# A graph layer with 64 experts on one core: degree counting over 320 rows in place of 444, a first expert pass of 48 node tiles, expert sizes in steps of 16

## The chip, the cores and the metric

The kernel runs on one core of one Trainium2 chip. The metric is the device time of one execution in microseconds (us); less is better. Engines are named as in the profile: PE is TensorE's matrix unit (PEld its weight loads), DVE is VectorE, ACT is ScalarE, POOL is GpSimd, and SP is SyncE, which here only issues DMAs. An indirect DMA that POOL issues fetches or stores 128 rows of a tensor in HBM by a list of 128 indices.

## The reference

There are 12,500 nodes with 256 features, and 212,500 edges, sorted by their destination. The layer sums each node's neighbours (with weights from the degrees), passes the sum and the node through two matrices, sends each node to the two best of 64 experts, adds what these return, normalizes each column over all nodes, adds the input and normalizes each row.

```python
def _forward(feats, W_gc, b_gc, W_res, b_res, Wg, bg, w1, b1, w2, b2, gamma, beta, src, dst):
    deg_out = jnp.clip(segment_sum(ones, src), 1.0)
    deg_in = jnp.clip(segment_sum(ones, dst), 1.0)
    h = feats * rsqrt(deg_out)[:, None]
    m = segment_sum(h[src], dst) * rsqrt(deg_in)[:, None]
    x = m @ W_gc + b_gc + feats @ W_res + b_res            # 12500 x 256
    vals, idx = top_k(x @ Wg + bg, 2); gates = softmax(vals)
    # expert e on its nodes: gelu(x @ w1[e] + b1[e]) @ w2[e] + b2[e],  w1: 256x512, w2: 512x256
    y = x + sum of gate * expert(x) over the node's two experts
    return (y - mean(y, 0)) * rsqrt(var(y, 0) + eps) * gamma + beta
result = layernorm(x + _forward(x, ...))
...
```

All matrix products are in float32; only counts and comparisons are in bfloat16.

## The kernel before

**Start.** The degrees by destination are counted from the sorted list, the features are scaled by them and written to HBM as `h_d`. Before that, POOL makes constants: `lane_b`, `diff`, ..., then `from_a` by one iota for each distinct size in `TOKENS_A`, then `cen`, a block of zeros and `place`, from which DVE makes the first keys.

**Edges, in rows.** A row is 128 edges; there are `MC` = 1596. For each, POOL gathers 128 rows of `h_d` into one of 20 places of a ring (`row`, L763, the DMA on L767), DVE makes a 128x128 matrix of ones and zeros from the destinations (`one_hot`, L759, twelve rows ahead), and PE multiplies the two (L784). Twelve rows make a group, which is copied (L819), transposed (L834) and added to the sums `acc` (L857). All other work of this stage is put between the rows by hand: `at_row(c, f)` puts f behind row c, `later` puts it some rows on, `spread` distributes a list. So the order on every engine is fixed when the program is built, and each engine works through its own list in order. The stage is in two pieces: `go(0, CA)` with `CA` = `PA` x 12 = 528 rows, and, behind a branch that is not taken with these inputs, `go(CA, MC)`.

**Counting.** Within the first piece the out-degrees are counted, to see that they equal the in-degrees (the graph is symmetric). The 68 steps lie between row `COUNT_FROM` = 30 and `COUNT_TO` = `CA` - 54. Each step is two large comparisons on DVE (`compare` and `compare_b`, which call `hot`, L237), eight sign instructions on ACT (L1454) and 25 small matmuls on PE (L1459 and L1463, in lots of five rows). The comparisons write into two buffers in turn, so step k waits for the matmuls of step k-2. Between rows 62 and 281 DVE also packs lists of edges (`squeezing`).

**Node chains.** From row `CA` on, `begin_nodes` starts a chain for each two tiles of 128 nodes whose sums are complete, at least `BETWEEN` = 12 rows apart: dense product (L929, L934), best two experts, ranks among the nodes of an expert, and entries into the expert's list (L1062, into the PSUM tile `tab`). The expert outputs of the first `TA` = 44 tiles ("A nodes") come from pass A, those of the other 54 ("B nodes") from pass B. A nodes are written to `xa_d`, B nodes to `xb_d`.

**Pass A.** When the chains of the A nodes are through, `pass_a` sorts the experts by their number of nodes and spreads their work over the rest of the rows, up to `END_A` - 20 = row 1564. `TOKENS_A` has, for the 64 ranks, a size in units of `TU` = 32 nodes that the expert of that rank is taken to have; if an expert had more, a slow path would run. `parts_a` cuts sizes over `MOST_A` = 224 into parts. For each tile of 128: a gather on POOL (L1236), a transposition (L1249), the hidden layer (L1272, gelu L1283), the product (L1300), and a store to `oa_d`. Both passes use 128 columns of PE per tile however few nodes the last tile has.

**Pass B** comes after the last row, in an order that the framework's scheduler sets. `pieces_of(TOKENS_B, 4)` cuts each expert into parts of at most 4 tiles. For each part: POOL gathers the tiles (`gather`, L1696), PE transposes them (L1711), DVE copies that (L1715), PE makes the hidden layer (L1724, 16 records a part), ACT the gelu (L1728), PE the product (L1751, 8 records a tile), DVE adds the bias and scales (L1756, L1761), and POOL stores each tile to `z_d` (L1762). Gathers run three parts ahead (`AHEAD`). The weights of an expert are 1 MB, loaded into one of three buffers (L1686). Beside the first 44 parts stand the A nodes: for each tile, two gathers from `oa_d` (`added`, L1784) that DVE adds in (L1790), and every four tiles a transposition (L1800). `order_of` sorts the experts for either pass; among its small instructions are DVE memsets that lay out the sizes.

**End.** The B nodes' outputs are read back from `z_d` in units of four tiles (`NODES_B`, L1926) and added on PE (L1945, L1947) with the statistics on DVE (L1953). Then come the normalization and the stores.

Of the kernel before, what the change touches and what calls it, by code (L numbers as in the profile page):

```python
# [19 lines left out]
P = 128  # L20
# [34 lines left out]
LAST = M - HE - (NL - 1) * L  # L55
PA = 44
CA = PA * GR
# [24 lines left out]
def last_node(g):  # L82
    return min(center(g) + SL, N - W)


TU = 32

TA = 44
NA = TA * P
ZR = NP - NA  # L90
TOKENS_A = [
    13, 12, 11, 10, 10, 9, 9, 9, 9, 8, 8, 8, 8, 8, 8, 8, 8, 7, 7, 7, 7, 7, 7, 7, 7, 6, 6, 6, 6,
    6, 6, 6, 6, 5, 5, 5, 5, 5, 5, 5, 5, 5, 5, 5, 5, 5, 4, 4, 4, 4, 4, 4, 4, 4, 4, 4, 3, 3, 3, 3,
    3, 3, 3, 3,
]
TOKENS_B = [
    16, 15, 14, 13, 13, 12, 12, 11, 11, 10, 10, 10, 10, 10, 10, 9, 9, 9, 9, 9, 9, 8, 8, 8, 8, 8,
    7, 7, 7, 7, 7, 7, 7, 7, 7, 7, 6, 6, 6, 6, 6, 6, 6, 5, 5, 5, 5, 5, 5, 5, 5, 5, 4, 4, 4, 4, 4,
    4, 4, 4, 4, 4, 4, 4,
]  # L100
MOST_A = 7 * TU
RPE = CAP // P
# [38 lines left out]
def gnn_moe_kernel(  # L141
# [209 lines left out]
    for b in sorted(set(TOKENS_A), reverse=True):  # L351
        n = TOKENS_A.count(b)
        GP.iota(
            from_a[:, a : a + n], pattern=[[b * TU, n]], base=sum(TOKENS_A[:a]) * TU,
            channel_multiplier=0, allow_small_or_imprecise_dtypes=True,
        )
# [739 lines left out]
    parts_a = pairs_of(TOKENS_A, MOST_A)  # L1096
    END_A = MC - 12

    def order_of(one, total, sizes, ord_p, exp, over):
# [12 lines left out]
        V.tensor_add(pos[:, 0:1], pos[:, 0:1], pos[:, 1:2])  # L1112
        V.tensor_scalar(perm, lane[:E, :E], pos[:, 0:1], None, op0=ALU.is_equal)
        V.tensor_copy(pos[:, 0:1], part[:E])
        V.tensor_scalar_min(pos[:, 1:2], cnt, float(CAP))
        for k in range(2):
            T.matmul(ord_p[:, k], pos[:, k : k + 1], perm, start=True, stop=True)
        V.tensor_copy(exp[:, 0], ord_p[:, 0])
        V.tensor_scalar_mul(exp[:, 1], ord_p[:, 0], float(RPE))
        room, more = one([1, E]), one([1, E])  # L1120
        at = 0
        for b in sorted(set(sizes), reverse=True):
            V.memset(room[:, at : at + sizes.count(b)], float(b * TU))
            at += sizes.count(b)
        V.tensor_tensor(more, ord_p[:, 1], room, op=ALU.is_gt)
        V.tensor_reduce(over, more, axis=AX.X, op=ALU.add)
        return junk, cnt, perm
# [5 lines left out]
    def pass_a(t):  # L1133
# [7 lines left out]
        def one(shape):  # L1141
# [5 lines left out]
        junk, cnt, perm = order_of(  # L1147
            one, total_a, TOKENS_A, shut(t)[:1, : 2 * E].rearrange("p (k e) -> p k e", k=2),
            exp_a, over_a,
# [474 lines left out]
    with tc.manual_schedule(engines=EVERY):  # L1624
# [42 lines left out]
    order_of(  # L1667
        lambda shape: one.tile(shape, F32, name=f"ord{next(names)}"), total, TOKENS_B,
        banks[0][:1, : 2 * E].rearrange("p (k e) -> p k e", k=2), exp_b, over_b,
# [5 lines left out]
    with ExitStack() as stack:  # L1675
# [29 lines left out]
        def turn(xg):  # L1705
# [3 lines left out]
            for k in range(n):  # L1709
                for c in range(2):  # L1710
                    T.transpose(  # L1711
                        xtp[:, c, k * P : (k + 1) * P], xg[k][:, c * P : (c + 1) * P], ident
                    )
            xT = two.tile([P, 2, 4 * P], F32, name="xT")
            V.tensor_copy(xT[:, :, : n * P], xtp[:, :, : n * P])  # L1715
            return xT

        def hidden(w, xT, m):
            w1 = w[:, : 2 * H].rearrange("p (c h) -> p c h", h=H)
            h1 = two.tile([P, 4, 4 * P], F32, name="h1")  # L1720
            for j in range(4):
# [142 lines left out]
        with tc.If(nc.values_load(over_n[0:1, 0:1]) > 0):  # L1864
            with tc.For_i(0, E, 1) as e:
                w, bb = load(e)
                at = two.tile([P, RPE], I32, name="at")
                V.tensor_copy(at, slot_a[:, bass.ds(e * RPE, RPE)])
                for b in range(0, RPE, 4):
                    h1 = hidden(w, turn(gather(at[:, b : b + 4], 4, xa_d)), 4 * P)  # L1870
                    for k, r, yo in products(w, bb, h1, 4 * P):
                        nc.sync.dma_start(og_d[bass.ds(e * CAP + (b + k) * P, P)], yo)
# [19 lines left out]
            with tc.For_i(0, E, 1) as e:  # L1892
# [4 lines left out]
                V.tensor_copy(second, snd[:, bass.ds(e * RPE, RPE)])  # L1897
                for b in range(0, RPE, 4):
                    g = gather(at[:, 0, b : b + 4], 4)
                    gb = gates_of(g, second[:, b : b + 4])  # L1900
                    outputs(w, bb, at[:, 1, b : b + 4], gb, hidden(w, turn(g), 4 * P), 4 * P)

# [201 lines left out]
```

## Time and profile before

| | |
|---|---|
| median of 3 runs | 3065.71 us (3063.93 to 3073.05) |
| the profiled execution | 3071.5 us, of which the span from first to last instruction is 3069.7 us |
| granted TensorE clock over the span | 0.936 |
| busy | PE 2510.7 us (82%), PEld 1867.0 (61%), DVE 1644.5 (54%), ACT 729.5 (24%), POOL 2048.1 (67%) |
| first gather of a row, last gather of a row | 97.38 us, 2299.11 us |
| first matmul of the hidden layer in pass B | 2355.92 us |

So the span has four stretches: the start up to 97 us, the rows up to 2299 us, pass B up to 2901 us, and the end. A line of a group has the line of the program, engine, operation, what is written and read, and the count; then busy time and the mean duration in ns of one; then the idle time of the engine just before such instructions and what ended it. The matmuls' ends are modelled, so two neighbours may overlap in a timeline; from the start of one to the start of the next is the pace. Each matmul instruction in float32 shows as two records. A line of windows has the stretch, its length, the busy time and count of each engine, the granted clock, the share of the DMA engines and GB/s.

### The profile page before, as it was taken

The page shows a single profiled execution, that of the slowest core. Times are in us where ns is not written, and L with a number is a line of the kernel's source. Part 1 is how long each engine was busy: PE and PEld are TensorE (multiplying, and loading weights), DVE is VectorE, ACT ScalarE, POOL GpSimd, SP SyncE. Part 2 cuts the span into 40 slices and gives each one's busy share as a digit, 9 for nine tenths or more (in the row PEclk, how much of TensorE's full clock was granted, in tenths as well). Part 3 has the DMA queues.
Part 4 walks back from the last instruction along what each step waited for, and adds up shares of the span by engine and source line. Part 5 has one row for each costly group of instructions (what it writes and reads, how often), then busy time and mean ns, then how long its engine had stood idle before and what let it go on. Part 6 is the DMA issues. An engine that isn't in the chain of part 4 may idle for free. (4 is left out here: it accounts for less than half of the span.)

```text
span 3069.7 us, 42189 instructions
## 1 busy us (share of the span) xinstructions
PE 2510.7 (82%) x12984; PEld 1867.0 (61%) x13053; DVE 1644.5 (54%) x6062; ACT 729.5 (24%) x2126; POOL 2048.1 (67%) x2114
## 2 busy tenths in 40 slices
PE   2477777777688887899998988999895899989895
PEld 2254455454465554667777766677772577877795
DVE  8567775554378776454444343444455544444247
ACT  2023334331111111222222122122220121222246
POOL 0577777777777777777777777777774667765200
PEclk9979988997799998999999999999997999999998
DMA  8833333344565555556666777777864566787768
GB/s 282 253 95 102 103 101 107 109 114 116 183 189 150 146 141 156 153 178 184 193 193 201 203 211 196 209 229 239 252 204 129 166 209 206 252 258 230 259 208 277
DMA packets 288735, 566.53 MB, mean 185 GB/s; under 512 B 56759, under 2 KB 194967, under 8 KB 280307
## 3 DMA queue, kind: packets, MB, share of 16 engines
q0 software_dynamic: 99728, 271.07, 30.8%
q1 hardware_dynamic: 175063, 279.59, 28.8%
q10 hardware_dynamic: 13708, 13.06, 1.4%
q8 instruction: 107, 1.75, 0.2%
q14 instruction: 129, 1.06, 0.1%
HBM read 495.77 MB, written 67.76 MB: 184 GB/s over the span
## 5 line engine op out<-in xcount | busy, mean ns | idle before, releaser
L767 POOL DMA_INDIRECT ring<-h_d,src_col x1596 | 1565.0, 981 | 577.8 <-issue 428.2
L784 PE MATMUL p<-ring,o 128*128 128x257 f32 (+1 forms) x3192 | 1054.3, 432 | 311.2 <-DMA ring<-h_d,src_col 257.8
L784 PEld LDWEIGHTS p<-ring,o 128*128 128x128 f32 x3192 | 565.3, 205 | 544.3 <-DMA ring<-h_d,src_col 328.9
L759 DVE TENSOR_SCALAR o<-lane,rel 128x128 f32<-128x128 f32 x1596 | 399.5, 297 | 224.7 <-PE p L784 223.7
L1283 ACT ACTIVATE acc<-p,acc 128x128 f32<-128x128 f32 (+4 forms) x332 | 128.3, 387 | 734.2 <-PE p L1272 451.8
L237 DVE TENSOR_TENSOR acc<-bank,acc 125x2450 bf16<-125x2450 bf16 (+1 forms) x136 | 185.1, 1361 | 197.0 <-PE bank L1459 189.6
L1751 PE MATMUL yp<-w,h 128*128 128x256 f32 (+3 forms) x1136 | 263.9, 383 | 17.8 <-DVE yo L1756 17.8
L1307 DVE TENSOR_TENSOR acc<-yp_a,acc 128x256 f32<-128x256 f32 (+3 forms) x120 | 50.2, 418 | 426.2 <-PE yp_a L1300 422.8
L1272 PE MATMUL p<-acc 128*128 128x128 f32 (+4 forms) x1328 | 238.1, 302 | 4.6 <-ACT s L819 0.9
L1724 PE MATMUL hp<-xT,w 128*128 128x128 f32 (+12 forms) x1024 | 227.2, 374 | 15.2 <-DVE xT L1715 14.1
L1272 PEld LDWEIGHTS p<-acc 128*128 128x128 f32 x1328 | 209.4, 193 | 47.5 <-ACT acc L1283 25.5
L1300 PE MATMUL yp_a<-acc 128*128 128x256 f32 (+3 forms) x960 | 236.7, 391 | 0.0
L1751 PEld LDWEIGHTS yp<-w,h 128*128 128x128 f32 (+3 forms) x1136 | 189.7, 174 | 70.8 <-DVE yo L1756 21.9
L1454 ACT ACTIVATE acc<-lane_b,acc 125x128 bf16<-125x128 bf16 x544 | 168.3, 389 | 239.0 <-PE bank L1463 149.3
L1728 ACT ACTIVATE h<-hp,w 128x128 f32<-128x128 f32 (+12 forms) x256 | 117.2, 460 | 393.1 <-PE hp L1724 334.6
L1724 PEld LDWEIGHTS hp<-xT,w 128*128 128x128 f32 x1024 | 171.4, 194 | 63.0 <-issue 25.3
L1762 POOL DMA_INDIRECT z_d<-yo,tables x142 | 137.8, 971 | 94.0 <-DVE gate L1738 37.6
L1300 PEld LDWEIGHTS yp_a<-acc 128*128 128x128 f32 (+3 forms) x960 | 164.0, 175 | 47.0 <-issue 8.4
L1696 POOL DMA_INDIRECT xg<-xb_d,tables x142 | 137.2, 966 | 72.4 <-PE xtp L1711 33.9
L819 ACT COPY s<-p 128x257 f32<-128x257 f32 (+1 forms) x133 | 49.7, 374 | 491.6 <-PE p L784 401.0
L1459 PEld LDWEIGHTS <-acc 125*128 125x128 bf16 x1156 | 86.9, 105 | 102.2 <-issue 59.1
L1236 POOL DMA_INDIRECT acc<-xa_d,tables x120 | 114.9, 958 | 36.6 <-issue 30.2
(350 smaller groups left out, 3205.1 us busy)
## 6 DMA issues: line engine op xcount, KB each, us to landing
w<-in_wpack SPq DMA_DIRECT2D x64, 1026.0 KB
acc<-in_wpack SPq DMA_DIRECT2D x128, 512.0 KB
ring<-h_d,src_col POOLq DMA_INDIRECT x1596
tables<-h_d SPq DMA_DIRECT2D x105, 128.0 KB
zt<-z_d SPq DMA_DIRECT2D x26, 512.0 KB
acc<-acc_d SPq DMA_DIRECT2D x14, 896.0 KB
xt<-in_x ACTq DMA_DIRECT2D x48, 256.0 KB
z<-in_x SPq DMA_DIRECT2D x12, 1024.0 KB
```

What stands on the lines that cost most here:

```text
L237: V.tensor_tensor(o.rearrange("p k (a b) -> p k a b", b=2), lane_b[:p, None, :n] .rearrange("p k (a b) -> p k a b", b=2) .to_broadcast([p, ...
L759: o_last[u] = V.tensor_scalar(o_of[u][:, j], lane, rel[:, c : c + 1], None, op0=ALU.is_equal)
L767: i = GP.indirect_dma_start(out=r[:, k, :D], out_offset=None, in_=h_d, in_offset=bass.IndirectOffsetOnAxis(ap=src_col[:, c : c + 1], axis=0),)
L784: i = T.matmul(p_of[g][:, :n], o_of[v][:, m], r[:, k, :n], start=j == 0, stop=j == GR - 1)
L1272: T.matmul(hp, w1[:, c, j * P : (j + 1) * P], xT[:, c, :m], start=c == 0, stop=c == 1,)
L1283: S.activation(h1[:, j, :m], hp_of.pop((q, j)), AF.Gelu, bias=b1_a[i % 2][:, j : j + 1])
L1300: T.matmul(y, h1[:, j, k * P : k * P + n], w2[:, j], start=j == 0, stop=j == 3)
L1454: S.activation(s_los[k % 2][:, j], lane_b[:EP], AF.Sign, bias=nbs[u % 2][:, i, j : j + 1])
L1696: GP.indirect_dma_start(out=g, out_offset=None, in_=of, in_offset=bass.IndirectOffsetOnAxis(ap=at[:, k : k + 1], axis=0),)
L1724: T.matmul(hp[:, :m], w1[:, c, j * P : (j + 1) * P], xT[:, c, :m], start=c == 0, stop=c == 1,)
L1751: T.matmul(yp[:r], h1[:, j, k * P : k * P + r], w2[:, j], start=j == 0, stop=j == 3,)
L1762: st = GP.indirect_dma_start(out=z_d, out_offset=bass.IndirectOffsetOnAxis(ap=at[:r, k : k + 1], axis=0), in_=yo[:r], in_offset=None,)
```

## The change

- `PA` goes from 44 to 34, and so `CA` from 528 to 408. Counting lies between rows 30 and 354, and the branch and the first node chains come at row 408.
- `TA` goes from 44 to 48 tiles, so there are 6144 A nodes in place of 5632, and 50 B tiles in place of 54. `END_A` - 20 is row 1596, the end of the rows, in place of 1564.
- `TU` goes from 32 to 16, with new tables of sizes. `TOKENS_A` sums to 12,944 places (12,448 before) for 12,288 entries (11,264 before), in 90 parts and 127 tiles (83 and 120). `TOKENS_B` sums to 13,344 places (15,232) for 12,712 entries (13,736), in 66 parts and 129 tiles (64 and 142).
- Pass B's parts have at most 3 tiles (`WIDE`), not 4, and its tiles `xT` and `h1` shrink with that. An expert with four tiles is now cut into two and two.
- The sizes for the test on overflow are laid out by POOL at the start, into the new tile `room` (38 small memsets), in place of DVE memsets in `order_of`. POOL's `from_a` takes 18 iotas in place of 11.
- The slow path works in lots of 2 tiles in place of 4; it does not run with these inputs.

```diff
-PA = 44
+PA = 34
-TU = 32
-TA = 44
+TU = 16
+TA = 48
 TOKENS_A = [
-    13, 12, 11, 10, 10, 9, 9, 9, 9, 8, 8, 8, 8, 8, 8, 8, 8, 7, 7, 7, 7, 7, 7, 7, 7, 6, 6, 6, 6,
...
+    26, 24, 23, 22, 21, 19, 19, 18, 18, 17, 17, 17, 17, 17, 16, 16, 16, 16, 15, 15, 15, 15, 15,
...
 TOKENS_B = [
-    16, 15, 14, 13, 13, 12, 12, 11, 11, 10, 10, 10, 10, 10, 10, 9, 9, 9, 9, 9, 9, 8, 8, 8, 8, 8,
...
+    27, 25, 23, 23, 22, 21, 20, 19, 18, 18, 18, 18, 17, 17, 17, 16, 16, 16, 16, 15, 15, 15, 15,
...
-MOST_A = 7 * TU
+MOST_A = 14 * TU
+WIDE = 3
...
+    room = route.tile([1, 2, E], F32)
...
+    for k, sizes in enumerate((TOKENS_A, TOKENS_B)):
+        for b in set(sizes):
+            a, n = sizes.index(b), sizes.count(b)
+            GP.memset(room[:, k, a : a + n], float(b * TU))
...
-    END_A = MC - 12
+    END_A = MC + 20
...
-        room, more = one([1, E]), one([1, E])
-        at = 0
-        for b in sorted(set(sizes), reverse=True):
-            V.memset(room[:, at : at + sizes.count(b)], float(b * TU))
-            at += sizes.count(b)
+        more = one([1, E])
...
-            xT = two.tile([P, 2, 4 * P], F32, name="xT")
+            xT = two.tile([P, 2, WIDE * P], F32, name="xT")
-            h1 = two.tile([P, 4, 4 * P], F32, name="h1")
+            h1 = two.tile([P, 4, WIDE * P], F32, name="h1")
-        parts = pieces_of(TOKENS_B, 4)
+        parts = pieces_of(TOKENS_B, WIDE)
```

The lines of the changed program lie 2 to 6 further on: L767 is L773 there, L784 is L790, L1236 is L1238, L1272 is L1274, L1300 is L1302, L1696 is L1698.

Where the instructions stand, first on POOL from the last gather of pass A to the first store of pass B. Before (`ring` is a row, `acc<-xa_d` a tile of pass A, `xg` a tile of pass B, `co` a tile of A outputs, `z_d` a store):

```order
L1236 DMA acc<-xa_d,tables 128x258
L767 DMA ring<-h_d,src_col 128x256 x59
L1638 IOTA rank 128x512
L1643 IOTA to 128x512
L1784 DMA co<-oa_d,pos_a 128x256 x3
L1696 DMA xg<-xb_d,tables 128x258 x17
L1784 DMA co<-oa_d,pos_a 128x256 x3
L1696 DMA xg<-xb_d,tables 128x258 x4
L1784 DMA co<-oa_d,pos_a 128x256 x3
L1762 DMA z_d<-yo,tables 79360x256
```

And after the change:

```order
L1238 DMA acc<-xa_d,tables 128x258
L773 DMA ring<-h_d,src_col 128x256 x27
L1640 IOTA rank 128x512
L1645 IOTA to 128x512
L1786 DMA co<-oa_d,pos_a 128x256 x3
L1698 DMA xg<-xb_d,tables 128x258 x11
L1786 DMA co<-oa_d,pos_a 128x256
L1698 DMA xg<-xb_d,tables 128x258 x3
L1786 DMA co<-oa_d,pos_a 128x256 x2
L1698 DMA xg<-xb_d,tables 128x258 x3
L1786 DMA co<-oa_d,pos_a 128x256 x4
L1764 DMA z_d<-yo,tables 78336x256
```

The last gather of pass A has moved from row 1537 to row 1569 (its first from row 855 to row 903), and the first store of pass B stands behind 27 DMAs of that pass in place of 30, because its first part has two tiles in place of four.

Second, PE behind the last dense product of two tiles, where the last rows are multiplied. Before, nothing of pass A is left there (`p` written from `ring` comes from a row; `bank` belongs to the node chain):

```order
L934 MATMUL bank_122<-wcat,xT 128x320 x2
L784 MATMUL p_123<-ring,o 128x257 x2
L996 LDWEIGHTS before
L996 MATMUL bank_121<-both,before 128x64
L997 LDWEIGHTS ones_b
L997 MATMUL bank_121<-both,ones_b 128x64
L996 LDWEIGHTS before
L996 MATMUL bank_122<-both,before 128x64
L997 LDWEIGHTS ones_b
L997 MATMUL bank_122<-both,ones_b 128x64
L784 MATMUL p_123<-ring,o 128x257 x2
```

After the change the hidden layer (L1274) and the products (L1302) of pass A stand between these rows:

```order
L940 MATMUL bank_123<-wcat,xT 128x320 x2
L790 MATMUL p_124<-ring,o 128x257
L1302 MATMUL yp_a<-acc 96x256 x4
L1274 MATMUL p_125<-acc 128x96 x2
L790 MATMUL p_124<-ring,o 128x257
L1002 LDWEIGHTS before
L1002 MATMUL bank_122<-both,before 128x64
L1003 LDWEIGHTS ones_b
L1003 MATMUL bank_122<-both,ones_b 128x64
L1002 LDWEIGHTS before
L1002 MATMUL bank_123<-both,before 128x64
```

One product of pass A, four matmuls of 96 rows, now stands behind the very last row.

More of the change, by code (lines that the diff above doesn't have):

```diff
@@ L91 @@
 TOKENS_A = [
-    13, 12, 11, 10, 10, 9, 9, 9, 9, 8, 8, 8, 8, 8, 8, 8, 8, 7, 7, 7, 7, 7, 7, 7, 7, 6, 6, 6, 6,
-    6, 6, 6, 6, 5, 5, 5, 5, 5, 5, 5, 5, 5, 5, 5, 5, 5, 4, 4, 4, 4, 4, 4, 4, 4, 4, 4, 3, 3, 3, 3,
-    3, 3, 3, 3,
[3 rows of a table added]
 ]
 TOKENS_B = [
-    16, 15, 14, 13, 13, 12, 12, 11, 11, 10, 10, 10, 10, 10, 10, 9, 9, 9, 9, 9, 9, 8, 8, 8, 8, 8,
-    7, 7, 7, 7, 7, 7, 7, 7, 7, 7, 6, 6, 6, 6, 6, 6, 6, 5, 5, 5, 5, 5, 5, 5, 5, 5, 4, 4, 4, 4, 4,
-    4, 4, 4, 4, 4, 4, 4,
-]
-MOST_A = 7 * TU
[3 rows of a table added]
+]
+MOST_A = 14 * TU
+WIDE = 3
 RPE = CAP // P
@@ L1096, in gnn_moe_kernel, with order_of @@
     parts_a = pairs_of(TOKENS_A, MOST_A)
-    END_A = MC - 12
-    def order_of(one, total, sizes, ord_p, exp, over):
+    END_A = MC + 20
+    def order_of(one, total, room, ord_p, exp, over):
         junk, cnt, pos, perm = one([E, E]), one([E, 1]), one([E, 2]), one([E, E])
@@ L1147, in pass_a @@
         junk, cnt, perm = order_of(
-            one, total_a, TOKENS_A, shut(t)[:1, : 2 * E].rearrange("p (k e) -> p k e", k=2),
+            one, total_a, room[:, 0], shut(t)[:1, : 2 * E].rearrange("p (k e) -> p k e", k=2),
             exp_a, over_a,
@@ L1667, in gnn_moe_kernel @@
     order_of(
-        lambda shape: one.tile(shape, F32, name=f"ord{next(names)}"), total, TOKENS_B,
+        lambda shape: one.tile(shape, F32, name=f"ord{next(names)}"), total, room[:, 1],
         banks[0][:1, : 2 * E].rearrange("p (k e) -> p k e", k=2), exp_b, over_b,
@@ L1868, in gnn_moe_kernel @@
                 V.tensor_copy(at, slot_a[:, bass.ds(e * RPE, RPE)])
-                for b in range(0, RPE, 4):
-                    h1 = hidden(w, turn(gather(at[:, b : b + 4], 4, xa_d)), 4 * P)
-                    for k, r, yo in products(w, bb, h1, 4 * P):
+                for b in range(0, RPE, 2):
+                    h1 = hidden(w, turn(gather(at[:, b : b + 2], 2, xa_d)), 2 * P)
+                    for k, r, yo in products(w, bb, h1, 2 * P):
                         nc.sync.dma_start(og_d[bass.ds(e * CAP + (b + k) * P, P)], yo)
@@ L1897, in gnn_moe_kernel @@
                 V.tensor_copy(second, snd[:, bass.ds(e * RPE, RPE)])
[L1898 to L1901, printed above, removed]
+                for b in range(0, RPE, 2):
+                    g = gather(at[:, 0, b : b + 2], 2)
+                    gb = gates_of(g, second[:, b : b + 2])
+                    outputs(w, bb, at[:, 1, b : b + 2], gb, hidden(w, turn(g), 2 * P), 2 * P)
     with ExitStack() as stack:
```

4 rows, old and new, of tables (TOKENS_A, TOKENS_B) are left out of this document.

## The prediction

> **What bounds the kernel now.** I read the windows first, to see which engine has no time to spare in each stretch, then the timeline at the seams, then the groups by form for durations. Two windows of the rows and two of pass B:
>
> ```profile
> core 0: us, PE busy (x) PEld busy (x) DVE busy (x) ACT busy (x) POOL busy (x), PEclk, DMA share, GB/s
> ...
> 300.00:400.00 100.00, 73.37 (x467) 48.93 (x466) 72.83 (x166) 32.20 (x103) 76.22 (x79) 0.90 0.36 103
> ...
> 2000.00:2100.00 100.00, 93.39 (x463) 70.19 (x467) 41.11 (x195) 22.60 (x71) 76.10 (x79) 0.98 0.73 215
> ...
> 2500.00:2600.00 100.00, 97.17 (x443) 70.75 (x442) 43.60 (x114) 20.49 (x40) 70.98 (x74) 1.00 0.68 206
> ...
> 2700.00:2800.00 100.00, 93.54 (x493) 78.65 (x492) 43.61 (x113) 24.78 (x58) 63.69 (x66) 0.98 0.75 240
> ```
>
> POOL issues 79 gathers in each 100 us of the rows, early and late. Its 76 us "busy" looks like spare time, but is none: the group of the gathers and the timeline at the last of them say why.
>
> ```profile
> L767 POOL DMA_INDIRECT ring<-h_d,src_col x1596 | 1565.0, 981 | 577.8 <-issue 428.2 <-DVE o L759 91.7 <-PE p L784 14.9
> ```
>
> ```profile
> 2297.86 0.94 POOL L767 DMA_INDIRECT ring<-h_d,src_col  x1 [0.30 <-issue]
> ...
> 2299.11 0.95 POOL L767 DMA_INDIRECT ring<-h_d,src_col  x1 [0.30 <-issue]
> ...
> 2309.51 1.05 POOL L1638 IOTA rank<- 128x512 f32 x1 [9.46 <-PE p L784]
> ```
>
> One gather takes 0.95 us and 0.30 us of issue: 1.25 us from start to start. 1596 + 120 of them are 2145 us of the 2202 us from first to last (97.38 to 2299.11). Nothing but "issue" holds POOL up for long, so the rows are bound by the number of gathers. In pass B, PE is busy for 93 to 97 us in 100, but POOL with 74 DMAs is near its 80 too.
>
> **The change part by part.** The profiled execution took 3071.5 us, 5.8 above the median of 3065.7; I sum differences and set them off against the median.
>
> *The start.* POOL's seven more iotas and 38 memsets stand ahead of `place`, for which DVE's first key waits.
>
> ```profile
> 0.25 0.10 POOL L2091 MEMSET const-float32-0.0<- 128x1 f32 x1 [0.25 <-issue]
> 0.28 0.10 POOL L2091 MEMSET const-float32-1.0<- 128x1 f32 x1
> ...
> 2.01 1.08 POOL L353 IOTA from_a<- 64x1 f32 x11
> ...
> 3.76 1.95 POOL L388 IOTA rel<- 125x1716 bf16 x1
> ```
>
> ```profile
> 6.59 1.93 DVE L418 SCALAR_TENSOR_TENSOR lines<-lines,rel 125x1700 f32<-125x1700 int32 x1 [5.00 <-DMA lines<-in_dst]
> ```
>
> Iotas: 7 x 0.098 = 0.7 us. Memsets start 0.03 us apart and last 0.10, so 38 are 1.1 to 3.8 us. `place` is ready at 5.71 and the key starts at 6.59 on a DMA, so 0.9 us are covered: +0.9 to +3.6; I take +1, since successive memsets overlap in these rows. The DVE memsets that go from `order_of` were placed in a wait and give nothing.
>
> *Counting in 324 rows, not 444.* The same 68 steps. DVE's share is the question, because in rows 62 to 281 `squeezing` runs beside it.
>
> ```profile
> L237 DVE TENSOR_TENSOR acc<-bank,acc 125x2450 bf16<-125x2450 bf16 (+1 forms) x47 | 64.0, 1362 | 52.1 <-PE bank L1459 49.6 <-PE bank L1463 2.1
> ```
>
> That is 64.0 of DVE's 145 busy us in the 200 us from 200 to 400. The steps come 6.53 / 4.76 = 1.37 times as densely, which adds at most 0.37 x 64 / 2 = 12 us and about 1 us of digits per 100: DVE goes from 73 to 86, and PE likewise. Both stay below 100, and the ring's 20 rows (25 us) cover short delays. I take 0 for it; if DVE falls behind, the price is among the rivals. The early branch lets 15 chains start 120 rows sooner, and nobody waits for them: POOL's pace does not depend on it.
>
> A gather can be held up by DVE:
>
> ```profile
> 135.25 1.71 POOL L767 DMA_INDIRECT ring<-h_d,src_col  x1 [0.30 <-issue]
> 137.26 3.98 POOL L767 DMA_INDIRECT ring<-h_d,src_col  x1 [0.30 <-PE p L784]
> ```
>
> The second lasts 3.0 us longer than the normal 0.95. If such losses went by the row, 120 fewer rows of counting would give some back: counting shows about 79 gathers per 100 us where 80 would fit, so 1% of 150 us, -1.5 us. If they go by the DVE instruction, it is 0, since no comparison is removed. I take 0. The Trainium skill (SBUF — State Buffer, "Who interferes with whom") says that a DVE instruction in a two-port mode and GpSimd block each other for a whole instruction; by that rule the loss goes by the instruction, so the sum has 0 and not -1.5. The long gather above agrees with it in kind.
>
> *Pass A with 127 tiles.* Seven more gathers on POOL, where the rows are bound: 7 x 1.25 = +8.8 us. PE's part of pass A grows by 6% and is spread over 666 rows, not 682 (last and first gather), so its density per row grows by 8%. From 1300 to 2250:
>
> ```profile
> L784 PE MATMUL p<-ring,o 128*128 128x257 f32 x1260 | 378.2, 397 | 75.5 <-DMA ring<-h_d,src_col 54.7 <-ACT ring L779 16.1 <-ACT acc L1283 3.2
> L1300 PE MATMUL yp_a<-acc 128*128 128x256 f32 (+3 forms) x886 | 219.2, 392 | 0.0
> L1272 PE MATMUL p<-acc 128*128 128x128 f32 (+4 forms) x1196 | 217.4, 305 | 4.2 <-ACT s L819 0.9 <-ACT acc L1283 0.3
> ```
>
> 8% of 437 us is 35 us in these 950, and PE waits 75.5 us there for rows: it still has slack, and POOL stays the bound. 0 beyond the gathers.
>
> *The end of the rows.* Pass A now runs to the last row. Before, it was over at 2285, and PE then worked off rows that lay ready:
>
> ```profile
> 2286.43 2.33 PE L784 MATMUL p<-ring,o 128*128 128x257 f32 x10
> ...
> 2288.82 5.38 PE L784 MATMUL p<-ring,o 128*128 128x257 f32 x24
> ```
>
> 34 records are 17 rows, done in 7.7 us where POOL takes 21.3 us to fetch as many: PE made up 13.6 us just ahead of the last chains. After the change there is no such stretch, and one product stands behind the last row (four matmuls, about half of the 3.62 us that two such tiles take further below, 1.8). What PE is late there is handed on, since the last two chains are one step after another. Bounds 0 (if chains leave gaps) and 15.4; I take +13, near the upper end, because the order shows pass A between all of the last rows.
>
> *Pass B.* Starts in the timeline give PE's pace:
>
> ```profile
> 2365.97 3.62 PE L1751 MATMUL yp<-w,h 128*128 128x256 f32 x16
> ...
> 2402.50 6.18 PE L1724 MATMUL hp<-xT,w 128*128 128x448 f32 x16
> ...
> 2408.51 1.04 PE L1711 MATMUL xtp<-ident,xg 128*128 128x128 f32 x8
> ```
>
> ```profile
> 2889.38 1.95 PE L1724 MATMUL hp<-xT,w 128*128 128x128 f32 x16
> 2891.17 0.38 PE L1711 MATMUL xtp<-ident,xg 128*128 128x128 f32 x2
> 2891.39 1.89 PE L1751 MATMUL yp<-w,h 128*128 128x256 f32 x8
> 2893.11 1.95 PE L1724 MATMUL hp<-xT,w 128*128 128x128 f32 x16
> ```
>
> A hidden layer of 448 columns takes 6.01 us to the next start, 13.4 ns a column; 128 columns take 1.79 us, which I take as the least also for 112 and 96. A tile takes 0.22 us to transpose and 1.72 to 1.81 for the product, I take 2.01 for both. Beside the first parts, 0.22 us per A tile (L1800). So PE needs 500 us before and 452 after: 1888 columns less are 25 us, 13 tiles less 26, and 9 parts under the least size and 4 more A tiles give 3 back. POOL: 2 x 142 + 88 = 372 DMAs before, 2 x 129 + 96 = 354 after, by 1.255: 467 and 444 us. Now by part, with what lasts longer, PE or POOL (two DMAs a tile, and two more with an A tile): before, 18 parts of two tiles have POOL on top (135.5 us against 126.5), after, 29 of two tiles and 3 of three (248.5 against 227.9). The sums of the longer one are 509 and 473 us. Measured, the first hidden layer starts at 2355.92 and the last product, at 2899.43, lasts 1.9: 545 us, 1.07 times the sum. So -36.6 x 1.07 = -39 us. The first part has two tiles less to fetch: 2 x 1.25 and 0.5 of a copy, -3 us. Against it stands the last stretch, now 16 parts with 1 MB of weights each and not 12:
>
> ```profile
> 2880.00:2890.00 10.00, 10.00 (x70) 9.36 (x69) 3.68 (x10) 3.40 (x10) 1.95 (x2) 1.00 0.95 331
> ```
>
> The DMA engines are 95% busy with such parts; I take +3 us. Pass B: -39 us. Bounds: POOL alone -22.6 x 1.07 - 3 = -27, PE alone -48 x 1.09 - 3 = -55; I take the middle, since parts of either kind make it up.
>
> *The end.* One unit of four B tiles less:
>
> ```profile
> 2929.51 0.70 DVE L1953 BATCH_NORM_STATS2 stat<-q 128x6 f32<-128x512 f32 x1 [1.52 <-PE q L1947]
> ...
> 2931.74 0.70 DVE L1953 BATCH_NORM_STATS2 stat<-q 128x6 f32<-128x512 f32 x1 [1.52 <-PE q L1947]
> ```
>
> Half a unit per 2.22 us, and DVE waits for PE each time: -4.4 us. All else there is as before.
>
> *Sum:* +1 + 8.8 + 13 - 39 - 4.4 = -20.6, so 3065.7 - 20.6 = 3045 us.
>
> **The rivals.** *Counting does not fit into 324 rows (slower).* In the group above each comparison waits 1.1 us for PE (52.1 / 47), because step k needs the matmuls of step k-2. I took it that DVE, far ahead, only waits out its spare time. If the wait stays with each comparison, DVE needs 145.4 us per 155 rows, of which comparisons are some 62: with 1.37 times these 1.09 us a row, and 2 x 1.1 / 4.76 = 0.46 more, 1.55 against POOL's 1.25. Over 324 rows that is 97 us late, less the ring's 25: +72, and 3117 us. It decides from the point where a row takes 1.25 + 25 / 324 = 1.33 us, a wait of 0.57 us per comparison. For it: DVE and PE at 86 wait for each other. Against it: PE has nothing else to do in the wait, and its own load stays under 90.
>
> *POOL alone bounds pass B (no change).* Then pass B gives -27 and all is -8.6: 3057 us. For it: 32 parts of 48 have POOL on top. Against it: the stretch from 2500 to 2600 still shows PE at 97 and POOL 6 DMAs short of its pace.
>
> *PE alone bounds pass B (faster still).* -55 gives -36.6: 3029 us. For it: that same window. Against it: POOL's own sum, which this cannot undercut for long.
>
> That an expert outgrows its size and the slow path runs is excluded by the inputs: the largest counts that I worked out from the reference leave at least two places in every rank of both new tables.
>
> **How the numbers follow.** Forecast 50%, between 3034 and 3056 for itself; POOL alone 20%; PE alone 15%; counting too slow 10%; 5% for something on either side. The measurement tells 0.3%, 9 us, from no change. Faster by more: forecast, PE alone, a little of the rest, 66%. Within: POOL alone and some, 22%. Slower: counting and the rest, 12%. The range reaches down to the sum with -55 in pass B and a tail of +6 (-43.6: 3022) and up to POOL alone with the upper ends of start and tail (+3.6, +15.4: -3.6, 3062), and some 6 us beyond, into the beginning of a late count: 3022 to 3068.
>
> **What would show it right or wrong.** First gather near 98 us; 79 gathers per 100 us between rows 30 and 354 (below 77, counting is too slow); last gather near 2309; the first hidden layer of pass B some 20 us later than 2356, not more; 506 us from there to the last product; 4.4 us less from there to the end. Wrong would be: POOL waiting for `p` in the rows, a tail over 25 us longer, or pass B at 520 us with POOL issuing 79 DMAs in 100 us throughout.

## The result, and the profile after

| | us | runs | ratio to before, 95% interval |
|---|---|---|---|
| before | 3067.2 | 6 | |
| after | 3044.7 (3039.0 to 3052.0) | 6 | 0.9926 [0.9908, 0.9944] |
| forecast | 3045 (3022 to 3068) | | |

The change is worth 22 us by the medians, as forecast, but not by the forecast's own sum. The two profiled executions are 3071.5 and 3040.7 us, 30.8 us apart, which is more than the medians are: this execution of before lies above its median, this one of after below. The 30.8 us, cut at the first and last gather of a row, the first hidden layer of pass B and its last product:

| stretch | before | after | difference | forecast |
|---|---|---|---|---|
| start, to the first gather | 97.4 | 98.5 | +1.2 | +1 |
| rows, first to last gather | 2201.7 | 2198.3 | -3.4 | +8.8 |
| last gather to first hidden layer | 56.8 | 62.2 | +5.4 | +13 and -3 |
| pass B, to the end of its last product | 545.4 | 514.6 | -30.8 | -39 and +3 |
| end | 168.4 | 165.3 | -3.1 | -4.4 |

First the windows of after that answer to those of before (length, then busy time and count of PE, PEld, DVE, ACT, POOL, then granted clock, DMA share, GB/s):

```profile
300.00:400.00 100.00, 70.37 (x568) 50.86 (x567) 85.92 (x180) 41.60 (x137) 76.24 (x79) 0.91 0.35 105
2000.00:2100.00 100.00, 93.20 (x460) 69.01 (x459) 35.82 (x163) 21.57 (x67) 76.29 (x78) 1.00 0.71 212
2500.00:2600.00 100.00, 93.05 (x438) 74.47 (x437) 42.67 (x110) 22.81 (x48) 69.03 (x71) 0.97 0.69 231
2700.00:2800.00 100.00, 93.94 (x511) 72.51 (x510) 44.83 (x116) 23.19 (x58) 66.36 (x70) 0.97 0.75 245
```

In the rows DVE rose from 73 to 86 and POOL kept its 79 gathers: counting fits. PE did not rise to 86; it fell from 73.4 to 70.4, with 568 records for 467. In pass B PE is at 93 from 2500 to 2600, where it was at 97 before, with the granted clock at 0.97. The group of the gathers, and POOL at the last of them:

```profile
L773 POOL DMA_INDIRECT ring<-h_d,src_col x1596 | 1548.2, 970 | 577.1 <-issue 430.5 <-DVE o L765 90.8 <-PE p L790 18.6
```

```profile
2295.57 0.95 POOL L773 DMA_INDIRECT ring<-h_d,src_col  x1 [0.31 <-issue]
2296.82 0.95 POOL L773 DMA_INDIRECT ring<-h_d,src_col  x1 [0.30 <-issue]
2317.27 1.05 POOL L1640 IOTA rank<- 128x512 f32 x1 [19.50 <-PE p L790]
```

There are two differences from before. The mean gather is 970 ns and not 981, and the wait behind the last gather is 19.5 us and not 9.46: these are the rows' gain and the later end of the last rows' products. PE there, after:

```profile
2307.45 0.60 PE L790 MATMUL p<-ring,o 128*128 128x257 f32 x2
2307.88 1.89 PE L1302 MATMUL yp_a<-acc 128*96 128x256 f32 x8
2309.61 0.58 PE L1274 MATMUL p<-acc 128*128 128x96 f32 x4
2310.02 0.63 PE L790 MATMUL p<-ring,o 128*128 128x257 f32 x2
```

Before, 24 and 10 records of rows (L784) stood in one piece here; now each row has work of pass A behind it.

### The profile page after: what moved, and what is told of

It is laid out like the page before. It is cut to its first block, busy times and chain, and to the rows that moved or that the text cites. A ratio compares the mean times of both kernels' runs of the same rounds, so it can differ in the third digit from the quotient of the medians.

```text
span 3038.9 us, 42466 instructions
## 1 busy us (share of the span) xinstructions
PE 2467.3 (81%) x13105; PEld 1838.4 (60%) x13105; DVE 1638.8 (54%) x6025; ACT 731.7 (24%) x2167; POOL 2027.0 (67%) x2148
## 5 line engine op out<-in xcount | busy, mean ns | idle before, releaser
L773 POOL DMA_INDIRECT ring<-h_d,src_col x1596 | 1548.2, 970 | 577.1 <-issue 430.5
L790 PE MATMUL p<-ring,o 128*128 128x257 f32 (+1 forms) x3192 | 1053.7, 430 | 233.2 <-DMA ring<-h_d,src_col 181.7
L790 PEld LDWEIGHTS p<-ring,o 128*128 128x128 f32 x3192 | 558.2, 204 | 465.7 <-DMA ring<-h_d,src_col 266.7
L1285 ACT ACTIVATE acc<-p,acc 128x128 f32<-128x128 f32 (+8 forms) x360 | 137.0, 381 | 739.6 <-PE p L1274 443.5
L1309 DVE TENSOR_TENSOR acc<-yp_a,acc 128x256 f32<-128x256 f32 (+7 forms) x127 | 53.2, 419 | 403.6 <-PE yp_a L1302 400.0
L1274 PE MATMUL p<-acc 128*128 128x128 f32 (+8 forms) x1440 | 249.5, 296 | 7.3 <-ACT acc L1285 3.0
L1274 PEld LDWEIGHTS p<-acc 128*128 128x128 f32 x1440 | 221.8, 192 | 51.2 <-ACT acc L1285 33.7
L1753 PE MATMUL yp<-w,h 128*128 128x256 f32 (+7 forms) x1032 | 240.5, 383 | 9.1 <-DVE yo L1758 9.0
L1302 PE MATMUL yp_a<-acc 128*128 128x256 f32 (+7 forms) x1016 | 247.8, 388 | 0.0
L1726 PE MATMUL hp<-xT,w 128*128 128x112 f32 (+17 forms) x1056 | 212.6, 356 | 31.5 <-DVE xT L1717 30.6
L1726 PEld LDWEIGHTS hp<-xT,w 128*128 128x128 f32 x1056 | 177.1, 202 | 62.6 <-DVE xT L1717 34.8
L1461 PE MATMUL bank<-acc 125*128 125x98 bf16 x1156 | 101.0, 214 | 129.7 <-DVE acc L239 109.7
L1753 PEld LDWEIGHTS yp<-w,h 128*128 128x128 f32 (+7 forms) x1032 | 169.0, 171 | 58.4 <-DVE yo L1758 13.0
L1730 ACT ACTIVATE h<-hp,w 128x128 f32<-128x128 f32 (+16 forms) x264 | 112.8, 429 | 376.9 <-PE hp L1726 320.7
L1302 PEld LDWEIGHTS yp_a<-acc 128*128 128x128 f32 (+7 forms) x1016 | 168.9, 171 | 48.3 <-issue 9.1
L1764 POOL DMA_INDIRECT z_d<-yo,tables x129 | 124.1, 962 | 90.4 <-DVE gate L1740 41.3
L1698 POOL DMA_INDIRECT xg<-xb_d,tables x129 | 124.4, 965 | 50.2 <-issue 18.6
```

The source lines that it names most:

```text
L773: i = GP.indirect_dma_start(out=r[:, k, :D], out_offset=None, in_=h_d, in_offset=bass.IndirectOffsetOnAxis(ap=src_col[:, c : c + 1], axis=0),)
L790: i = T.matmul(p_of[g][:, :n], o_of[v][:, m], r[:, k, :n], start=j == 0, stop=j == GR - 1)
L1274: T.matmul(hp, w1[:, c, j * P : (j + 1) * P], xT[:, c, :m], start=c == 0, stop=c == 1,)
L1285: S.activation(h1[:, j, :m], hp_of.pop((q, j)), AF.Gelu, bias=b1_a[i % 2][:, j : j + 1])
L1302: T.matmul(y, h1[:, j, k * P : k * P + n], w2[:, j], start=j == 0, stop=j == 3)
L1461: T.matmul(deg, o_los[k % 2][:, j], o_his[k % 2][:, j], start=k + j == 0, stop=False)
```

## The experiments

Those called "after with" change the changed kernel, the others the kernel before. Each is compared with runs of the kernel before on the same chip, made beside it. "Lost" is the time from one gather to another beyond 1.2535 us for each gather between them (the pace of an undisturbed stretch), summed over the rows named. It varies a little from kernel to kernel even where nothing that bears on it differs, so 2 or 3 us more or less of it say nothing.

**The changed kernel again.**

> The changed kernel once more, as the measure for the other three. Theory: the gain is in pass B (-31 us in the trace) and in one unit less at the end (-4), and seven more gathers cost 8.8 us in the rows; that the rows came out 3.4 us shorter from first to last gather, not 8.8 longer, is chance: how many gathers happen to fall on a DVE instruction that holds POOL up. Then 0.993 of before again (3045 us), and the time lost beyond 1.25 us per gather in rows 30 to 354, 10.9 us in the profile of the changed kernel and 20.5 in that of the kernel before, comes out anywhere between these. Rival: denser counting itself gives POOL time back; then that loss is again near 11 us.

It took 3046.6 us, ratio 0.9938 [0.9923, 0.9952]. Pass B is 513.1 us, the stretch ahead of it 66.0, and the gathers of rows 30 to 354 lose 10.8 us (10.9 in the first profile, 20.6 before). So these differences belong to the kernel, not to one execution.

**After with counting over 444 rows.**

```diff
-PA = 34
+PA = 44
```

> The changed kernel with PA = 44 again: counting over rows 30 to 474 and node chains from row 528, all else as changed. Theory: POOL's pace does not depend on where counting and chains lie, and pass A starts where it did, so nothing is lost: within 0.3% of the changed kernel (3036 to 3054 us). Rival (counting over fewer rows is where gathers are gained): about 10 us more than the changed kernel, 3055 us, and a loss beyond 1.25 us per gather near 20 us in the counting rows.

It took 3054.4 us, ratio 0.9953 [0.9941, 0.9965], 7.7 us more than the changed kernel beside it. The intervals of the two ratios overlap, but the trace says where it is: rows 30 to 354 lose 20.3 us again, and all else is within 2 us of the changed kernel's run beside it. My expectation that PA is worth nothing, and that the smaller loss after was chance, is out. With PA the same as before, this run also shows the seven more gathers of pass A by themselves: its rows take 2210.8 us, 9.1 more than before, where +8.8 was forecast.

**The kernel before with PA = 34 alone.** This asks the same from the other side.

```diff
-PA = 44
+PA = 34
```

> The kernel before with PA = 34 alone, again. By the prediction (denser counting costs and gives nothing) the time is that of before in the same call, within 0.2%. By the theory that the rows get back what the gathers lose while lists are packed, the lost time in rows 30 to 354 falls from 20.6 to about 11 us and the time by as much, ratio 0.997.

It took 3059.9 us, ratio 0.9974 [0.9961, 0.9986]: 8 to 10 us less than before. Pass B (548.6) and the end (168.2) are within 3 us of before; the rows take 2186.6 us for 2201.7, and rows 30 to 354 lose 12.0 us. That is 8.6 of the rows' 15.1 us; most of the rest lies behind row 474 and is not explained. The window from 142 to 462 us, in which the lists are packed beside counting, of before and then of this kernel:

```profile
142.00:462.00 320.00, 234.25 (x1411) 155.85 (x1412) 225.39 (x510) 94.27 (x301) 246.84 (x241) 0.85 0.35 100
```

```profile
142.00:462.00 320.00, 218.21 (x1770) 155.20 (x1771) 268.97 (x559) 127.49 (x415) 245.06 (x247) 0.94 0.35 102
```

The gathers in this window, and in the one from 462 to 550 us, where packing is over and counting goes on, of before:

```profile
L767 POOL DMA_INDIRECT ring<-h_d,src_col x241 | 248.0, 1029 | 73.5 <-issue 64.0 <-PE bank L1459 2.7 <-PE bank L1463 2.7
...
L767 POOL DMA_INDIRECT ring<-h_d,src_col x70 | 67.7, 968 | 21.3 <-issue 19.8 <-PE bank L1459 0.6 <-PE bank L1463 0.6
```

And of the kernel with PA = 34:

```profile
L767 POOL DMA_INDIRECT ring<-h_d,src_col x247 | 246.1, 996 | 75.2 <-issue 66.4 <-PE bank L1459 3.0 <-PE bank L1463 2.4
...
L767 POOL DMA_INDIRECT ring<-h_d,src_col x71 | 67.6, 953 | 21.6 <-issue 18.6 <-PE bank L1459 1.5 <-PE bank L1463 0.3
```

With more of DVE's work in the window, 269 us for 225, a gather lasts 996 ns and not 1029, and six more of them fit. So the loss does not go by DVE's busy time, and not by the row of counting either: rows 354 to 474, which still count in the kernel before, lose 0.5 us. It goes with the work on the lists of edges, whose large DVE operations have 105 partitions (marking from row 3, packing from row 62). Lines of before show it: a gather that starts under a comparison (L237) keeps its 0.95 us, one that starts under an operation of packing (L689) lasts longer, and the long gather that the prediction quotes started at row 28 under such an operation (L656), 3.7 us before the first comparison:

```profile
203.01 1.44 DVE L237 TENSOR_TENSOR acc<-bank,acc 125x2450 bf16<-125x2450 bf16 x1 [1.17 <-PE bank L1459]
203.23 0.95 POOL L767 DMA_INDIRECT ring<-h_d,src_col  x1 [0.30 <-PE bank L1459]
...
204.36 0.68 DVE L689 TENSOR_SCALAR tab<-tables 105x512 int32<-105x512 int32 x1
...
204.48 1.45 POOL L767 DMA_INDIRECT ring<-h_d,src_col  x1 [0.30 <-issue]
```

```profile
136.73 3.52 DVE L656 TENSOR_TENSOR_SCAN lines<-lines 105x1616 f32<-105x1616 bf16 x1
```

All 254 gathers of rows 30 to 283, by what DVE does when they start; "longer" means by over 0.06 us beyond 0.95, and the last column sums that:

| DVE | gathers before, after | of them longer | longer by, us |
|---|---|---|---|
| an operation of 105 partitions is running | 50, 51 | 35, 28 | 16.3, 9.6 |
| none is, but one starts within 0.95 us | 73, 93 | 10, 4 | 3.2, 0.9 |
| a comparison is running, and no such operation follows | 39, 42 | 0, 0 | 0, 0 |
| all else | 92, 68 | 2, 3 | 0.5, 0.5 |

Rows 0 to 29, with marking and no comparison yet, lose 7.8 us before and 7.9 after. So a comparison alone holds no gather; what denser counting changes is when gathers meet the other work: as many start under such an operation, but fewer of them, and by less, are held. This is read from what overlaps; no run leaves the work on the lists out. In the three kernels with PA = 44 (before, this page's PA = 44 and the sizes in steps of 16 below) rows 30 to 354 lose 20.6, 20.3 and 17.3 us, in the seven with PA = 34 between 10.8 and 12.4. The Trainium skill (SBUF — State Buffer, "Who interferes with whom") says that the order of issue, not the shape of an operation, tells which of DVE and GpSimd blocks the other. The first two rows of the table agree (35 of 50 against 10 of 73). Why the order falls out better with denser counting stays open.

**After with pass A ending 32 rows earlier.**

```diff
-    END_A = MC + 20
+    END_A = MC - 12
```

> The changed kernel with END_A = MC - 12, so that pass A ends 32 rows before the last row as it did before the change. Theory: PE then makes up its delay ahead of the last chains; the last row is multiplied about 9 us behind its gather and not 19, and the time falls by about 10 us, to 3035 us; POOL's rows stay as long, since PE still has about 20 us of waits for rows in the 950 us from 1300 to 2250. Rival: with 5% more of pass A per row PE becomes the bound, gathers wait for the row matmuls, and the time is not less: 3045 us or more.

It took 3037.9 us, ratio 0.9904 [0.989, 0.9918], 8.7 us less than the changed kernel beside it (0.9938 [0.9923, 0.9952]; the intervals are apart). Its PE and POOL at the last rows:

```profile
2286.88 2.34 PE L790 MATMUL p<-ring,o 128*128 128x257 f32 x10
...
2289.27 5.38 PE L790 MATMUL p<-ring,o 128*128 128x257 f32 x24
```

```profile
2297.90 0.95 POOL L773 DMA_INDIRECT ring<-h_d,src_col  x1 [0.30 <-issue]
2309.79 1.05 POOL L1640 IOTA rank<- 128x512 f32 x1 [10.94 <-PE p L790]
```

PE catches up again, in the same two pieces of 10 and 24 records as before, the wait behind the last gather falls from 19.5 to 10.9 us, and pass B begins 54.6 us behind the last gather and not 66.0. Pass B itself is 517.1 us, 4 more than in the run beside it, which is not explained. The rows (2199.4) and their gathers are as in the changed kernel, so pass A loses nothing by the shorter stretch. This is the fastest version of those that compute the whole layer.

**After with one of the two gathers and additions for an A node in pass B.** The second expert's output of the A nodes is left out.

```diff
-            for k in range(2):
+            for k in range(1):
```

> The changed kernel with one gather from the A outputs per A node tile in pass B and not two (the second expert's output of the A nodes is left out of the result): 48 POOL DMAs and DVE additions fewer beside the first 48 parts, no change for PE. Theory (each part lasts as long as the longer of PE and POOL): the sum over the parts falls from 473 to 452 us, and by 1.07 pass B takes 22 us less, 493 us from the first hidden layer to the last product; 3023 us in all. Rival, POOL alone: 48 x 1.25 = 60 us less, 455 us, 2985 in all. Rival, PE alone: no change, 515 us, 3045 in all.

It took 3000.4 us, ratio 0.9778 [0.9764, 0.9792]. Pass B is 469.0 us, 44 less than the 513.1 of the run beside it: twice what the longer of PE and POOL gives (22), and three quarters of POOL alone (60). PE alone, which gives nothing, is out.

**After with both gathers and one addition.** The second expert's output is left out here too, but POOL does all its work.

```diff
-                V.scalar_tensor_tensor(
+                if k == 0:
+                    V.scalar_tensor_tensor(
```

> The changed kernel with both gathers of an A tile's outputs in pass B, but only the first of the two added in by DVE (the second expert's output of these nodes is left out of the result), again. If POOL's DMAs gave the 45 us of the run with neither, pass B stays at 513 us and the time at 0.993 of before. If DVE's additions gave them, pass B falls to about 470 us and the ratio to 0.979.

It took 3033.9 us, ratio 0.9881 [0.9866, 0.9897]. Pass B is 506.9 us, 6 to 8 us less than in the changed kernel's two profiles. POOL's gathers of A outputs in this kernel, and in the one with a single gather:

```profile
L1786 POOL DMA_INDIRECT co<-oa_d,pos_a x96 | 91.8, 956 | 87.2 <-DMA co<-oa_d,pos_a 34.8 <-DVE tables L1826 29.2 <-issue 18.6
```

```profile
L1786 POOL DMA_INDIRECT co<-oa_d,pos_a x48 | 47.2, 982 | 53.0 <-DVE tables L1825 29.2 <-DVE cy L1792 8.1 <-DVE yo L1763 7.2
```

Without a reader, a buffer `co` is free only when the gather before into it has landed, and POOL waits 34.8 us for that, so the price of an addition is not separated cleanly. By this run 6 to 8 of the 44 us go with the additions alone, and the other 36 to 38 only when POOL's 48 gathers go too. The 6 to 8 us come from parts 17 to 32; the section on why takes that up.

**The kernel before with sizes in steps of 16 alone** (new tables for 44 A tiles, four tiles a part at most).

```diff
-TU = 32
+TU = 16
...
-MOST_A = 7 * TU
+MOST_A = 14 * TU
```

> The kernel before with sizes in steps of 16 alone, again: 117 tiles in pass A and not 120, 140 in pass B and not 142. By the sum over parts of the longer of PE and POOL pass B gives 12 us and the rows 3.8, ratio 0.995. POOL alone: 5 and 3.8 (0.997). PE alone: 16 and 3.8 (0.9935).

It took 3056.2 us, ratio 0.9953 [0.9939, 0.9966], 13.5 less than before. The rows are 5.1 us shorter and pass B 9.6 (535.8): between POOL alone (5) and PE alone (16), near the longer of the two (12). Rows 30 to 354 lose 17.3 us here.

**After with sizes in steps of 32** (48 A tiles, three tiles a part).

```diff
-TU = 16
+TU = 32
...
-MOST_A = 14 * TU
+MOST_A = 7 * TU
```

> The changed kernel with sizes in steps of 32 again, all else as changed: the tables then give the same 127 tiles in pass A and 129 in pass B, only fuller parts. If POOL alone bounds pass B, nothing changes: 3045 us. By the longer of PE and POOL it is 2.4 us more (474.8 for 472.6), by PE alone 6 us more (457.6 for 452.0). None of these is above 0.2%, so steps of 16 would be worth little beside the 48 tiles; over 3055 would show a cost that the sum does not have.

It took 3045.5 us, ratio 0.9918 [0.9902, 0.9934], no different from the changed kernel. With the same 127 and 129 tiles, pass B is 519.3 us, some 5 more than after; the start is 1 us shorter and the rows 2 to 3.5, and this cancels. At 48 A tiles the finer steps buy nothing that can be measured; that leaves the number of tiles as what counted. The 5 us of pass B are nearer to the 6 of PE alone than to the 2.4 of the longer one.

**Runs on another chip.** PA = 34 alone, steps of 16 alone, and the run with both gathers and one addition were made first on a second chip, where the kernel before took 3782.7 us (23 runs) and not 3068.

> The kernel before with PA = 34 alone: counting in 324 rows, the first chains at row 408, all else as before. By the prediction (denser counting costs and gives nothing) the time is that of before, 3068 us, within 0.2%. By the new theory, that POOL loses time by the row of counting, the lost time of the gathers in rows 30 to 354 falls from 20.6 to about 11 us, and the time by as much, to 3058 us.

> The kernel before with sizes in steps of 16 alone (44 A tiles, parts of at most four tiles, PA = 44): 117 tiles in pass A and not 120, 140 in pass B and not 142. By the sum over parts of the longer of PE and POOL (498.2 for 509.2) pass B gives 12 us and the rows 3.8: 3053 us. If POOL alone bounds pass B (2 x 2 DMAs of 1.255 us fewer) it gives 5 us: 3060. If PE alone does (485.6 for 500.1) it gives 16: 3048.

> The changed kernel with both gathers of an A tile's outputs in pass B, but only the first of the two added in by DVE; the second expert's output of these nodes is left out of the result. With one gather and one addition (the run before) pass B took 45 us less. If that came from POOL's DMAs, this run keeps pass B at 513 us and the time at 3045. If it came from DVE's additions (48 fewer of about 0.45 us, and the buffers that they free), pass B falls to about 470 and the time to 3000. Shares in between say how much each carries.

The ratios there were 1.0176 [1.014, 1.0213], 0.9971 [0.9954, 0.9988] and 0.9999 [0.9972, 1.0027]: PA = 34 alone, which gains 8 to 10 us on the first chip, costs 61 us there. They answer another question, since POOL's pace does not bound the rows on that chip. A stretch of pass A, of before on the first chip and of PA = 34 on the second:

```profile
1400.00:1800.00 400.00, 360.66 (x1783) 282.71 (x1798) 160.63 (x751) 89.08 (x288) 304.42 (x314) 0.98 0.68 195
```

```profile
1400.00:1800.00 400.00, 261.03 (x1174) 198.43 (x1173) 135.74 (x575) 57.97 (x188) 213.88 (x222) 0.82 0.43 122
```

```profile
L767 POOL DMA_INDIRECT ring<-h_d,src_col x190 | 182.2, 959 | 76.8 <-issue 54.0 <-remote 13.8 <-PE p L784 7.5
```

A gather costs the same 0.96 us, but 222 are issued where 314 were, and no engine is busier than two thirds of the time. The trace puts many of the waits down to "remote" or "issue", that is, to nothing that it records; what held that chip up is not known. The runs further up were made on the first chip or on one like it, where the kernel before took 3069.7 us.

**After with counting over 276 rows,** on the second chip too.

```diff
-PA = 34
+PA = 30
```

> The changed kernel with PA = 30: the 68 steps of counting in 276 rows (rows 30 to 306) and not 324, a step every 4.06 rows. If POOL loses by the row of counting, the lost time of the gathers falls by a further 1.5 to 2 us and the time is 3043 to 3046, the same or a little less. By the rival that counting does not fit, with DVE and PE alternating at 100%, POOL waits for the matmuls of rows and the time is over 3065 us; 276 rows x 1.254 us / 68 leaves 5.1 us a step, of which the two comparisons take 2.7 and the packing of lists beside them about as much, so this is near the point.

It took 549,736 us and tells nothing of the pace. Behind row 360 the program took the branch that is otherwise not taken, and the general path handled all edges:

```profile
L1587 PE MATMUL q<-o_c,r_c 128*128 128x128 f32 x261148 | 79716.7, 461 | 125140.9 <-DVE o_c L1583 118860.8
```

Which of the conditions sent it there was not tried. The point at which counting becomes too dense was therefore not found; 324 rows are not yet too few.

## Why the prediction was right

The total was right by luck: errors of opposite sign cancelled. In the changed kernel's two profiles (the second: start +1.1, rows -1.8, stretch ahead of pass B +9.2, pass B -32.3, end -1.2) the rows came out 11 to 12 us below the forecast; pass B came out 4 to 5 us above it and the end 1 to 3, and the stretch ahead of pass B 1 to 5 below. That is -25 and -31 for the forecast's -20.6, and the medians' -22.5 is nearer to it because the profiled execution of before lay 4 us above its median. Of the prediction's own signs, the last gather came at 2296.8 us and not near 2309, the first hidden layer 3 us later than before (8 in the second profile) and not 20, and pass B took 514.6 us and not 506.

*Start.* +1 was forecast, and +1.2 measured:

```profile
3.62 1.41 POOL L363 MEMSET room<- 1x3 f32 x38
```

38 memsets take 1.41 us, near the lower bound as assumed.

*Denser counting: the step that failed.* It was costed at 0, with -1.5 if losses went by the row. It gave some -9 us, shown from both sides (20.6 to 12.0 us lost with PA = 34 alone, back to 20.3 with PA = 44 in the changed kernel). The 0 came from taking the loss to go by the DVE instruction, at a fixed price; but the comparisons and the work on the lists have the same instructions in all these kernels, and the loss halves. It does go by the instruction in so far as the operations of 105 partitions hold gathers and the comparisons do not; what each costs depends on when a gather starts beside it. The long gather quoted in the prediction came before any comparison; I did not ask what it stood beside. What the prediction said of cover held: DVE reached 86, and POOL kept its pace. "PE likewise" to 86 did not. The granted clock went from 0.85 to 0.94 in the window above, so that PE needed 218 us for 1770 records where it had needed 234 for 1411. The Trainium skill (TensorE: Matmul & The Clock Gate, "Part 1: The HAM clock gate") says that the array's clock is throttled by default and that activity releases it; this pair of windows agrees in direction.

*The rival that counting does not fit* (3117 us) is out. It rested on a DVE that waits 1.1 us for PE ahead of each comparison whatever it has in hand. From 200 to 400 us, before and then after:

```profile
DVE acc L237 <- PE bank L1459: 49.6, 25, 4.1
```

```profile
DVE acc L239 <- PE bank L1461: 22.6, 39, 1.9
...
DVE acc L239 <- PE bank L1465: 3.3, 7, 0.9
```

With 1.37 times as many comparisons the wait halved: it was spare time, as the prediction took it.

*Seven gathers of pass A.* +8.8 stands (+9.1 in the run with PA = 44). The rows' -3.4 are +8.8, -9.7 in rows 30 to 354, and about -2.5 from small losses elsewhere, which are no more than such losses vary.

*The end of the rows.* The later start of pass B was put at +13 - 3 = +10; the six profiles of kernels with pass A to the last row and 48 A tiles have 62.2 to 66.0 us there for 56.8, which is +5 to +9. The mechanism is shown by the run that ends pass A earlier, and its price there is 7.6 to 11 us for the 13 forecast.

*Pass B, the mis-sized term.* -36 was forecast for this stretch, and -31 and -32 measured in the two profiles. The counts of tiles, parts and DMAs were right, and so was pricing the hidden layer by its columns (the description of the kernel, with 128 columns a tile for the last tile too, holds for the transposition alone). The factor of 1.07 on the sum of the longer one was not a constant. By part, from the start of one hidden layer to another, against the prediction's own prices:

| parts | PE | POOL | longer one | measured | measured / longer |
|---|---|---|---|---|---|
| before, first 16 | 189.8 | 173.2 | 189.8 | 210.4 | 1.11 |
| before, 17 to 32 | 132.4 | 133.0 | 134.1 | 143.6 | 1.07 |
| before, 33 to 44 | 83.1 | 90.4 | 90.4 | 93.5 | 1.03 |
| after, first 16 | 153.3 | 150.6 | 155.9 | 180.2 | 1.16 |
| after, 17 to 32 | 120.9 | 123.0 | 123.6 | 138.4 | 1.12 |
| after, 33 to 48 | 105.1 | 120.5 | 120.5 | 122.0 | 1.01 |
| one gather of two, first 16 | 153.3 | 130.5 | 153.4 | 166.4 | 1.08 |
| one gather of two, 17 to 32 | 120.9 | 102.9 | 120.9 | 119.4 | 0.99 |
| one addition of two, first 16 | 153.3 | 150.6 | 155.9 | 181.2 | 1.16 |
| one addition of two, 17 to 32 | 120.9 | 123.0 | 123.6 | 127.3 | 1.03 |

The loss is not set by how near PE and POOL are to each other: parts 17 to 32 have the same sums after and with one addition of two, and take 1.12 and 1.03; the first 16 of before, where the two are 9% apart, take 1.11. The first 16 parts as windows, of before, after, and with one gather of two:

```profile
2356.00:2566.00 210.00, 195.24 (x809) 136.90 (x810) 96.38 (x322) 39.56 (x70) 147.48 (x153) 0.97 0.61 187
```

```profile
2359.00:2539.00 180.00, 162.22 (x725) 121.79 (x726) 84.88 (x302) 34.78 (x70) 131.81 (x137) 0.95 0.61 199
```

```profile
2366.00:2532.00 166.00, 158.33 (x723) 119.88 (x724) 77.91 (x281) 34.87 (x70) 113.94 (x119) 0.97 0.64 201
```

After, PE's 153.3 us at full clock are 161 at the granted 0.95 (162 busy), and it stands idle for 18 us more; with POOL relieved it is idle for 8. Two thirds of the 18 us are a wait that the sum does not have: PE's hidden layer waits for DVE's copy `xT`, and DVE, which works through its list in order, stands ahead of that copy in an addition (`cy`) whose gather has not landed. One of these waits, after:

```profile
2380.67 0.49 DVE L1792 SCALAR_TENSOR_TENSOR cy<-co,cy 128x256 f32<-128x256 f32 x1 [6.82 <-DMA co<-oa_d,pos_a]
...
2381.85 0.69 DVE L1717 COPY xT<-xtp 128x512 f32<-128x512 f32 x1
...
2382.59 1.22 PE L1726 MATMUL hp<-xT,w 128*128 128x256 f32 x2 [7.67 <-DVE xT L1717]
```

The sums of these waits over the first 16 parts (us, times, longest), after and then with one gather of two:

```profile
DVE cy L1792 <- DMA co<-oa_d,pos_a: 28.0, 13, 6.8
...
PE hp L1726 <- DVE xT L1717: 12.1, 3, 7.7
```

```profile
DVE cy L1792 <- DMA co<-oa_d,pos_a: 8.2, 2, 6.3
...
PE hp L1726 <- DVE xT L1717: 7.5, 2, 6.7
```

So a POOL that is late delays PE through DVE, even where PE's own sum is as long. (Before, PE's 15 us of idle time in these parts are waits for another instruction of DVE, `yo`.) In parts 17 to 32 PE's idle time falls from 11 us after to none with one gather of two, and the granted clock goes from 0.95 to 1.00. With one addition of two, PE has no wait for the copy left in these parts, which fits their 1.03; its first 16 parts then wait for other gathers (`xg`) and gain nothing. No run moves the copies ahead of the additions, so how much of the factor that order makes is not shown. Neither rival holds alone: in this stretch POOL alone would have given -24 and PE alone -52 (the -27 and -55 hold the -3 of the stretch ahead), and taking 48 DMAs off POOL, with their additions, gave 44 us although PE needed as long as POOL already. The prediction scaled POOL alone by 1.07, though 545 is 1.17 times POOL's 467; by that it would be -26 and not -24 here, which changes no reading. The 3 us for the last stretch's weights did not show as a wait: from 2800 to 2870, after,

```profile
2800.00:2870.00 70.00, 69.04 (x463) 60.45 (x462) 26.10 (x71) 25.38 (x70) 22.82 (x24) 1.00 0.89 311
```

PE is busy for 69 of 70 us with the DMA engines at 0.89.

*The end.* -4.4 was forecast; -3.1 and -1.2 were measured in the two profiles; what took the rest is not known.

## What to carry to other kernels

Work spread to the very last row of a stretch takes away the slack in which a lagging engine catches up: leave the last rows free when a serial chain follows them (8.7 us here, for one constant). A sum over parts of the longer of two engines leaves out what a third engine between them passes on: here it was up to 16% short, and relief of the one that came late paid twice what the sum said. Ask what stands, in the list of the engine in between, ahead of the instruction that the other waits for. And ask of a loss beside which instructions it falls, not only how large it is: the gather quoted in the prediction, held before counting had begun, would have shown that the comparisons were not the cause.

## What the runs showed of the hardware that was not expected

A gather on POOL that starts while DVE runs an operation of 105 partitions on the lists of edges is mostly held up (35 of 50 in rows 30 to 283 before, by 16.3 us together); one that starts under a comparison, with no such operation behind it, is not (0 of 39). So gathers can be held less when DVE is busier (996 ns at 269 us of DVE in 320, 1029 at 225). PE's granted clock rose with denser counting, from 0.85 to 0.94, and more matmuls took less time (218 us for 1770 records, 234 for 1411). And on a second chip the same kernel took 3783 us for 3068, with gathers of the same 0.96 us and pauses on several engines at once that the trace puts down to nothing it records.
